# Layer 0 of a two-layer image kernel: real transposes, sums of squares on ScalarE, and another order of the stages in a slot

## The chip, the cores and the metric

The kernel runs on one core of a Trainium2 chip. A core has five engines that run their own instruction streams in order and wait for each other through semaphores: TensorE (PE: matmuls; PEld is its weight load), VectorE (DVE), ScalarE (ACT), GpSimd (POOL) and SyncE (SP, which here issues most of the DMAs). TensorE writes to PSUM, from where VectorE and ScalarE read; GpSimd works in SBUF. The metric is the device time of one execution in microseconds (us), lower is better.

## The reference, cut to what matters

Eight images of 128 x 128 positions with 128 channels go through two layers. Layer 0 is linear attention with a normalization at its end:

```python
qkv = jnp.einsum('bhwc,cf->bhwf', x, w_qkv)
q, k, v = jnp.split(qkv, 3, axis=-1)          # each (B, 4 heads, 32, N), N = 128*128
q = jax.nn.softmax(q, axis=-2) * inv_scale    # over the 32 of a head
k = jax.nn.softmax(k, axis=-1)                # over all N positions
context = jnp.einsum('bhdn,bhen->bhde', k, v)
attn = jnp.einsum('bhde,bhdn->bhen', context, q)
out = jnp.einsum('bhwf,fc->bhwc', attn, w_out) + b_out
mu = jnp.mean(out, axis=-1, keepdims=True)
var = jnp.mean(jnp.square(out - mu), axis=-1, keepdims=True)
out = (out - mu) * jax.lax.rsqrt(var + LN_EPS) * gamma + beta
return out + x
```

Layer 1 is a convolution followed by four selective scans, a gate, a normalization and a projection. The change doesn't touch it.

## The kernel before, in words

Three stages follow each other: `layer0` (the first 2350 us), `layer1_front` (the convolution) and `layer1_scan`, the longest. `layer0` writes two tensors to memory: its result x1, and zs, the gate of layer 1 (Silu of x times half of layer 1's input weights).

An image of layer 0 is cut into 32 groups of 512 positions (`NG`, four columns of 128). Two things are done to each image: `context(b)`, which makes the 128 x 128 context out of keys and values, and afterwards `attend(b)`, which runs the queries through it. `image(b)` interleaves `attend(b)` with `context(b + 1)`, so that all engines have work of both. Its loop runs over slots t; each slot calls each stage once, for a group that lags by a fixed number: `at(scale, t - 2)`, `at(query, t)` and so on, where a = t - 1 counts the groups of the next image. The loop runs 39 slots. There is an image -1 with a context alone, and image 7 with attention alone, in which the gates of the last two images (`gate_group`) run inside the slots; the other images' gates run as one burst after slot 0.

The order of the calls in a slot is the order of the instructions: `in_order` chains all instructions of an engine as they were written. So a stage that is called earlier stands earlier in the queue of every engine it uses, and an instruction that waits holds back all that is behind it on its engine.

The stages of a group (lines of the kernel before):

- query (L266 to L272): TensorE pq = wq * x; VectorE takes the maximum of each head (qm) and subtracts it (q).
- exponent (L275): ScalarE, exp of q in place. normalize (L280 to L282): VectorE sums and inverts (qs), GpSimd multiplies.
- through_wo (L288, L290): four pairs of matmuls that multiply q by Wo, position by position, which also turns positions onto the partitions' side; ScalarE copies pg to gt.
- through_context (L294 to L298): TensorE po = context * gt; VectorE adds the bias (o); ScalarE squares o (sq).
- variance (L302): VectorE sums the squares over the 128 channels, four sums a partition.
- scale (L308 to L313): GpSimd makes rstd out of the four sums, by a power of -0.5 (L310), and d, four diagonal matrices: the identity times rstd.
- turn (L321): TensorE multiplies o by d, four 128 x 128 blocks, which turns o and scales it at once. A matmul in fp32 is two instructions in the profile.
- finish (L325 to L330): ScalarE applies gamma and beta (x1t), GpSimd adds x in place, and every second group a DMA stores two groups.

And of the next image: key (L180, copied by ScalarE to k, L182), larger (L190 to L197: running maximum over four groups on VectorE), fold (every fourth group; L206: a transposition by TensorE, then on VectorE the maximum m, the correction a and the diagonal dg, L208 to L214), spread (L219: a matmul spreads the maximum over the partitions, pmx; L221: ScalarE's exp of a), value (L225, L226), subtract (L231, VectorE), raise_to (L234, ScalarE's exp), add (L240: four pairs of matmuls sum k times v in pc; every fourth group VectorE folds pc into total, L247).

PSUM tiles with the tag "ps" share six buffers in turn, seven tiles a slot in every fourth slot and six otherwise.

The order of a slot before:

```python
            at(scale, t - 2)
            at(finish, t - 3)
            at(query, t)
            at(through_wo, t - 1)
            at(exponent, t)
            ...
            at(turn, t - 2)
            at(spread, a - 1)
            at(variance, t - 1)
```

Of the kernel before, what the change touches and what calls it, by code (L numbers as in the profile page):

```python
# [16 lines left out]
P = 128  # L17
# [7 lines left out]
GW = 4  # L25
GN = GW * H
NG = W // GW
BK = 4
# [49 lines left out]
def layer0(ctx: ExitStack, tc, xT, w_qkv, w_out, b_out, gamma, beta, win, x1, zs):  # L78
# [19 lines left out]
    ident = const.tile([P, P], F32, name="ident")  # L98
# [40 lines left out]
    def group(b, g):  # L139
        return xs[b % 2][:, g * GW : (g + 1) * GW, :]  # L140
# [6 lines left out]
    def gate_group(b, g):  # L147

        v = group(b, g)
        if ORDER[b] % K >= 2:  # L150
            v = wp.tile([P, GW, P], F32, name="v", tag="o", bufs=3)
            nc.vector.tensor_copy(
                v, xs[b % 2].rearrange("p w h -> p h w")[:, g * GW : (g + 1) * GW, :]
            )
        for c in range(NC2):
            pz = ps.tile([P, GW, P], F32, name="pz", tag="ps")
            nc.tensor.matmul(pz, wz[:, c * P : c * P + P], v, start=True, stop=True)
            z = wp.tile([P, GW, P], F32, name="z", tag="k", bufs=7)
            nc.scalar.activation(z, pz, AF.Silu)
            dst = zs[ORDER[b], c][:, g * GN : g * GN + GN]  # L160
            nc.sync.dma_start(dst, z.rearrange("p w h -> p (w h)"))

    def gate(b):

        turned = ORDER[b] % K >= 2
        more = b + 2 < B
        for g in range(NG):
            gate_group(b, g)
            if more and not turned and g % 4 == 3:
                load(b + 2, [g // 4])  # L170
        if more and turned:
            load(b + 2)
# [88 lines left out]
    def attend(b):  # L261

        cn = ctxs[b % 2]
        qs, gs, os, vs, ys = {}, {}, {}, {}, {}

        def query(g):  # L266
            pq = ps.tile([P, GW * NH, HD], F32, name="pq", tag="ps")
            nc.tensor.matmul(pq, wq[:, 0:P], group(b, g), start=True, stop=True)
            qm = sm.tile([P, GW * NH, 1], F32, name="qm")
            nc.vector.tensor_reduce(qm, pq, AX.X, ALU.max)  # L270
            qs[g] = q = wp.tile([P, GW * NH, HD], F32, name="q", bufs=3)
            nc.vector.tensor_tensor(q, pq, qm.to_broadcast([P, GW * NH, HD]), ALU.subtract)  # L272

        def exponent(g):
            nc.scalar.activation(qs[g], qs[g], AF.Exp)  # L275

        def normalize(g):
            q = qs[g]
            t = sm.tile([P, GW * NH, 1], F32, name="qs")
            nc.vector.tensor_reduce(t, q, AX.X, ALU.add)  # L280
            nc.vector.reciprocal(t, t)  # L281
            nc.gpsimd.tensor_tensor(q, q, t.to_broadcast([P, GW * NH, HD]), ALU.mult)  # L282

        def through_wo(g):
            q = qs.pop(g).rearrange("p (w n) d -> p w (n d)", w=GW)
            pg = ps.tile([P, GW, P], F32, name="pg", tag="ps")
            for i in range(GW):
                nc.tensor.matmul(pg[:, i, :], q[:, i, :], wo, start=True, stop=True)  # L288
            gs[g] = gt = wp.tile([P, GW, P], F32, name="gt")
            nc.scalar.copy(gt, pg)  # L290

        def through_context(g):
            po = ps.tile([P, GW, P], F32, name="po", tag="ps")
            nc.tensor.matmul(po, cn, gs.pop(g), start=True, stop=True)  # L294
            os[g] = o = wp.tile([P, GW, P], F32, name="o", bufs=3)
            nc.vector.tensor_tensor(o, po, bb, ALU.add)  # L296
            vs[g] = sq = wp.tile([P, GW, P], F32, name="sq")
            nc.scalar.activation(sq, o, AF.Square)  # L298

        def variance(g):  # L300
            var = sm.tile([P, GW], F32, name="var")
            nc.vector.tensor_reduce(var, vs[g], AX.X, ALU.add)  # L302
            vs[g] = var

        def scale(g):

            var = vs[g]
            nc.gpsimd.tensor_scalar(var, var, 1.0 / P, EPS0, ALU.mult, ALU.add)  # L308
            rstd = sm.tile([P, GW, 1], F32, name="rstd")
            nc.gpsimd.tensor_tensor(rstd[:, :, 0], var, half, ALU.pow)  # L310
            vs[g] = d = wp.tile([P, GW, P], F32, name="d")
            i3 = ident.rearrange("p (o c) -> p o c", o=1)
            nc.gpsimd.tensor_tensor(  # L313
                d, i3.to_broadcast([P, GW, P]), rstd.to_broadcast([P, GW, P]), ALU.mult
            )

        def turn(g):
            o, d = os.pop(g), vs.pop(g)
            ys[g] = pt = ps.tile([P, GW, P], F32, name="pt", tag="ps")
            for i in range(GW):  # L320
                nc.tensor.matmul(pt[:, i, :], o[:, i, :], d[:, i, :], start=True, stop=True)  # L321

        def finish(g):
            y = wp.tile([P, GW, P], F32, name="x1t")
            nc.scalar.activation(y, ys.pop(g), AF.Identity, bias=gb[:, 1:2], scale=gb[:, 0:1])  # L325
# [6 lines left out]
        return query, exponent, normalize, through_wo, through_context, variance, scale, turn, finish  # L332

    def image(b):

        key = larger = fold = spread = value = subtract = raise_to = add = None
        query = exponent = normalize = through_wo = through_context = None
        variance = scale = turn = finish = None
        later = LATER if b >= 0 else 0
        if b + 1 < B:  # L340
            key, larger, fold, spread, value, subtract, raise_to, add = context(b + 1)
        if b >= 0:
            (query, exponent, normalize, through_wo, through_context, variance, scale, turn,
             finish) = attend(b)

        def at(stage, g):
            if stage is not None and 0 <= g < NG:
                stage(g)

        for t in range(later + NG + BK + 2):  # L350
            a = t - later
            at(scale, t - 2)
            at(finish, t - 3)
            at(query, t)
            if b == B - 1 and t < NG:
                gate_group(b - 1, t)
            at(through_wo, t - 1)
            if b == B - 1 and 4 <= t < NG + 4:
                gate_group(b, t - 4)
            at(exponent, t)  # L360
            at(subtract, a - BK - 1)
            at(raise_to, a - BK - 1)
            at(key, a)
            at(normalize, t)
            at(fold, a - 1)
            at(value, a - BK - 1)
            at(larger, a)
            at(through_context, t - 1)
# [841 lines left out]
```

## Time and profile before

| | |
|---|---|
| median of 3 runs | 9565.71 us (9555.7 to 9566.26) |
| profiled execution, span | 9556.3 us |
| layer 0 | about the first 2350 us |
| PE busy, whole span | 6281.6 us, 66% |
| DVE busy, whole span | 8129.7 us, 85% |
| ACT busy, whole span | 7202.0 us, 75% |
| POOL busy, whole span | 7192.2 us, 75% |

The profiled execution is told by its span, from its first instruction to its last. The span lies 9.4 us under the median of the runs, within 1 us of the fastest run. Shares over the whole span mix the three stages: in the scans VectorE and GpSimd are nearly always busy, in layer 0 TensorE is. What the change is worth is to be read from layer 0 alone.

In the profile, L321 is line 321 of the kernel; "pt<-d,o" is a tile written out of the tiles d and o; "128x512" is partitions by elements; "[1.29 <-DVE dg L214]" is idle time before an instruction and the one whose end released it. Matmuls are pipelined, so the step from start to start says more than the length of one.

### The profile page before, as it was taken

What the parts mean: (1) busy time and instruction counts of PE and PEld (TensorE: products, weight loads), DVE (VectorE), ACT (ScalarE), POOL (GpSimd) and SP (SyncE); (2) the same over time, 40 slices, a digit from 0 to 9 for tenths busy, and PEclk for the clock granted to TensorE, in tenths of its full rate; (3) what the DMA queues carried; (4) which work ended last, traced back from release to release, by engine and by line L of the source; (5) the groups of instructions that cost most, each with busy time, mean ns of one, the idle gap of its engine ahead of it and who ended that gap; (6) DMA issues with size and microseconds to landing.
All of it is one profiled execution on the core that took longest, in us unless ns stands there. A gap on an engine that the chain in (4) does not pass through costs nothing. (4 is left out here: it accounts for less than half of the span.)

```text
span 9556.3 us, 89734 instructions
## 1 busy us (share of the span) xinstructions
PE 6281.6 (66%) x24190; PEld 3101.4 (32%) x24352; DVE 8129.7 (85%) x8188; ACT 7202.0 (75%) x8288; POOL 7192.2 (75%) x4361
## 2 busy tenths in 40 slices
PE   8999999898977788777823544636345363543636
PEld 5556655554322233222300311404123040220403
DVE  6667765564988889888979999999999999999996
ACT  5556555567877788777878788888888888888884
POOL 3445544455665578776859999999999999999997
PEclk9999999999988899888955665757557585665857
DMA  2332233313476678987765957759487685867858
GB/s 91 135 133 81 95 133 132 133 71 140 172 266 232 229 262 247 266 263 269 243 204 165 257 174 207 240 174 269 154 228 219 186 260 165 244 190 198 245 165 212
DMA packets 1034807, 1851.21 MB, mean 194 GB/s; under 512 B 274852, under 2 KB 500772, under 8 KB 1026112
## 3 DMA queue, kind: packets, MB, share of 16 engines
q1 hardware_dynamic: 999488, 1711.23, 54.2%
q0 software_dynamic: 34816, 134.23, 7.3%
q8 instruction: 199, 3.26, 0.1%
q14 instruction: 304, 2.49, 0.1%
HBM read 1153.03 MB, written 692.12 MB: 193 GB/s over the span
## 5 line engine op out<-in xcount | busy, mean ns | idle before, releaser
L893 POOL TENSOR_TENSOR ubt<-ubt,sp 128x1024 f32<-128x1024 f32 x1024 | 2457.9, 2458 | 161.0 <-ACT sp L886 74.3
L882 PE MATMUL px<-rows,dtw 128*128 128x512 bf16 x1893 | 909.5, 573 | 2271.7 <-DVE y L943 1063.5
L515 POOL TENSOR_TENSOR tap<-tap 128x1024 f32<-128x1024 f32 x512 | 1206.1, 2367 | 640.1 <-ACT tap L513 517.9
L523 DVE SCALAR_TENSOR_TENSOR acc<-xb,cw,acc 128x1024 f32<-128x1024 f32 x1024 | 1320.6, 1290 | 52.7 <-ACT tap L513 0.9
L886 ACT ACTIVATE sp<-px 128x1024 f32<-128x1024 f32 x1024 | 1046.0, 1024 | 420.7 <-PE px L882 265.6
L951 POOL TENSOR_TENSOR y<-y,ubt 128x512 f32<-128x512 f32 x768 | 1160.0, 1557 | 142.9 <-DVE ubt L924 141.9
L505 PE MATMUL acc<-xi,wt 128*128 128x512 f32 x2048 | 952.2, 608 | 383.9 <-ACT ures L530 383.6
L903 DVE TENSOR_TENSOR_SCAN ubt<-px,ubt 128x1024 f32<-128x1024 f32 x512 | 1177.0, 2332 | 25.9 <-POOL ubt L893 19.2
L901 DVE TENSOR_TENSOR_SCAN ubt<-px,ubt 128x1024 f32<-128x1024 f32 x512 | 1178.3, 2332 | 14.1 <-POOL ubt L893 6.3
L882 PEld LDWEIGHTS <-dtw 128*128 128x128 bf16 x2048 | 163.9, 109 | 3066.2 <-issue 865.9
L890 ACT ACTIVATE px<-sp,sa 128x1024 f32<-128x1024 f32 x1024 | 1110.2, 1109 | 6.1
L513 ACT ACTIVATE tap<-xb,cw 128x1024 f32<-128x1024 f32 x768 | 834.0, 1139 | 68.1 <-POOL tap L515 67.8
L282 POOL TENSOR_TENSOR q<-q,qs 128x512 f32<-128x512 f32 x256 | 271.2, 1060 | 691.5 <-DVE qs L281 691.5
L886 ACT ACT_TABLE_LOAD x512 | 656.9, 1283 | 164.5 <-PE px L882 129.2
L505 PEld LDWEIGHTS acc<-xi,wt 128*128 128x128 f32 x2048 | 383.6, 192 | 928.3 <-ACT ures L530 486.1
L890 ACT ACT_TABLE_LOAD x512 | 656.9, 1283 | 9.2
L1016 PEld LDWEIGHTS px<-wg,z 128*128 128x128 f32 x4096 | 553.8, 218 | 118.6 <-issue 113.5
L909 PE MATMUL pc<-rows,csel 128*128 128x512 bf16 x1017 | 512.7, 585 | 88.9 <-DVE rstd L1004 79.9
L1016 PE MATMUL px<-wg,z 128*128 128x128 f32 x4096 | 554.1, 301 | 0.0
L478 PE MATMUL pxb<-xi,wi 128*128 128x512 f32 x1024 | 495.9, 606 | 4.3 <-ACT xb L487 4.3
L943 DVE TENSOR_TENSOR y<-y,px 128x1024 f32<-128x1024 f32 x384 | 468.7, 1221 | 14.7 <-DVE px L931 0.5
L298 ACT ACTIVATE sq<-o 128x512 f32<-128x512 f32 x256 | 161.2, 630 | 418.2 <-DVE o L296 416.9
(155 smaller groups left out, 15187.7 us busy)
## 6 DMA issues: line engine op xcount, KB each, us to landing
ubt<-ubs SPq DMA_DIRECT2D x512, 1024.0 KB
zs<-z SPq DMA_DIRECT2D x512, 256.0 KB
ubs<-ures SPq DMA_DIRECT2D x256, 512.0 KB
ubs<-turned SPq DMA_DIRECT2D x256, 512.0 KB
z<-zs SPq DMA_DIRECT2D x256, 512.0 KB
y<-gs POOLq DMA_DIRECT2D x128, 1024.0 KB, 10.5
rows<-xps SPq DMA_DIRECT2D x1536, 60.0 KB
xi<-x SPq DMA_DIRECT2D x120, 576.0 KB
```

Of the source, the lines that this page charges most:

```text
L505: nc.tensor.matmul(acc[:, s, :], wt[:, j, c, :], x, start=(j == 0), stop=(j == len(ON_PE) - 1))
L513: nc.scalar.activation(t, at(n, c, *d), AF.Copy, scale=cw[:, c, tap(*d) : tap(*d) + 1])
L515: nc.gpsimd.tensor_tensor(sums[n, c], sums[n, c], t, ALU.add)
L523: nc.vector.scalar_tensor_tensor(acc, at(n, c, *d), cw[:, c, tap(*d) : tap(*d) + 1], acc, ALU.mult, ALU.add)
L882: nc.tensor.matmul(p[:, hf * 512 : hf * 512 + 512], sl.dw[:, c * P : c * P + P], src, start=True, stop=True)
L886: nc.scalar.activation(t, da[n, c], AF.Softplus)
L890: nc.scalar.activation(da[n, c], sp[n, c], AF.Exp, scale=sa[:, sl.s, c : c + 1])
L893: nc.gpsimd.tensor_tensor(ubt[n][:, c, :], ubt[n][:, c, :], sp.pop((n, c)), ALU.mult)
L901: nc.vector.tensor_tensor_scan(e[:, ::-1], x[:, ::-1], e[:, ::-1], start, ALU.mult, ALU.add)
L903: nc.vector.tensor_tensor_scan(e, x, e, start, ALU.mult, ALU.add)
L951: nc.gpsimd.tensor_tensor(v[:, c], v[:, c], h[:, c], ALU.add)
L1016: nc.tensor.matmul(po[:, w, :], z[:, c, w * H : w * H + H], wg[:, c, :], start=(c == 0), stop=(c == NC2 - 1))
```

## The change

Four things in layer 0:

1. The squares: in place of one ScalarE instruction over 128 x 512 and a sum by VectorE (stage variance, which goes), four ScalarE instructions over 128 x 128, each of which also writes the sum of its squares to one column of var (accum_out). The squares themselves are written to a tile of one buffer that nobody reads.
2. The scaling: GpSimd multiplies o itself by rstd, in place, and makes no diagonal matrix.
3. The turn: TensorE transposes the four blocks of o (`nc.tensor.transpose`, a matmul in transpose mode against the identity) in place of multiplying them by d.
4. The order of the calls in a slot. TensorE's is now query, (spread), key, value, Wo, (fold), adding, context, turn. spread is called one slot later than before, right behind query. raise_to comes behind key and value, and through_wo behind all of these; add comes ahead of through_context.

ScalarE's queue in a slot was x1t, gt, exponent of q, exponent of k, copy of k, copy of v, square; it becomes x1t, exponent of q, copy of k, copy of v, exponent of k, gt, four squares. In image 7 it was x1t, two z, gt, two z, exponent, square; it becomes x1t, two z, exponent, gt, two z, four squares. GpSimd's queue and that of the DMAs keep their order.

```diff
-            vs[g] = sq = wp.tile([P, GW, P], F32, name="sq")
-            nc.scalar.activation(sq, o, AF.Square)
-
-        def variance(g):
-            var = sm.tile([P, GW], F32, name="var")
-            nc.vector.tensor_reduce(var, vs[g], AX.X, ALU.add)
-            vs[g] = var
+            sq = wp.tile([P, GW, P], F32, name="sq", bufs=1)
+            vs[g] = var = sm.tile([P, GW], F32, name="var")
+            for i in range(GW):
+                nc.scalar.activation(sq[:, i, :], o[:, i, :], AF.Square, accum_out=var[:, i : i + 1])
 
         def scale(g):
 
-            var = vs[g]
+            var = vs.pop(g)
             nc.gpsimd.tensor_scalar(var, var, 1.0 / P, EPS0, ALU.mult, ALU.add)
             rstd = sm.tile([P, GW, 1], F32, name="rstd")
             nc.gpsimd.tensor_tensor(rstd[:, :, 0], var, half, ALU.pow)
-            vs[g] = d = wp.tile([P, GW, P], F32, name="d")
-            i3 = ident.rearrange("p (o c) -> p o c", o=1)
-            nc.gpsimd.tensor_tensor(
-                d, i3.to_broadcast([P, GW, P]), rstd.to_broadcast([P, GW, P]), ALU.mult
-            )
+            o = os[g]
+            nc.gpsimd.tensor_tensor(o, o, rstd.to_broadcast([P, GW, P]), ALU.mult)
 
         def turn(g):
-            o, d = os.pop(g), vs.pop(g)
+            o = os.pop(g)
             ys[g] = pt = ps.tile([P, GW, P], F32, name="pt", tag="ps")
             for i in range(GW):
-                nc.tensor.matmul(pt[:, i, :], o[:, i, :], d[:, i, :], start=True, stop=True)
+                nc.tensor.transpose(pt[:, i, :], o[:, i, :], ident)
...
             at(query, t)
+            at(spread, a - 2)
             if b == B - 1 and t < NG:
                 gate_group(b - 1, t)
+            at(exponent, t)
+            at(subtract, a - BK - 1)
+            at(key, a)
+            at(value, a - BK - 1)
+            at(raise_to, a - BK - 1)
+            at(normalize, t)
+            at(larger, a)
             at(through_wo, t - 1)
             if b == B - 1 and 4 <= t < NG + 4:
                 gate_group(b, t - 4)
-            at(exponent, t)
-            at(subtract, a - BK - 1)
-            at(raise_to, a - BK - 1)
-            at(key, a)
-            at(normalize, t)
             at(fold, a - 1)
-            at(value, a - BK - 1)
-            at(larger, a)
+            at(add, a - BK - 2)
             at(through_context, t - 1)
-            at(add, a - BK - 2)
             at(turn, t - 2)
-            at(spread, a - 1)
-            at(variance, t - 1)
```

More of the change, by code (lines that the diff above doesn't have):

```diff
@@ L330, in finish @@
                 nc.sync.dma_start(x1[ORDER[b]][:, (g - 1) * GN : (g + 1) * GN], t)
-        return query, exponent, normalize, through_wo, through_context, variance, scale, turn, finish
+        return query, exponent, normalize, through_wo, through_context, scale, turn, finish
     def image(b):
@@ L337, in image @@
         query = exponent = normalize = through_wo = through_context = None
-        variance = scale = turn = finish = None
+        scale = turn = finish = None
         later = LATER if b >= 0 else 0
@@ L342, in image @@
         if b >= 0:
-            (query, exponent, normalize, through_wo, through_context, variance, scale, turn,
+            (query, exponent, normalize, through_wo, through_context, scale, turn,
              finish) = attend(b)
```

## The prediction

> **What bounds the kernel now.** I read the windows view by stage, then TensorE's timeline, then ScalarE's groups and timeline, then both engines in image 7. The change touches layer 0 alone, about the first 2350 of 9556 us.
>
> ```profile
> 2050.00:2355.00 305.00, 253.58 (x963) 136.34 (x961) 118.61 (x213) 235.11 (x335) 152.15 (x169) 0.98 0.37 140
> 300.00:600.00 300.00, 276.58 (x1240) 171.47 (x1240) 211.51 (x361) 180.00 (x314) 154.06 (x172) 0.98 0.30 114
> ```
>
> Columns: window, length, then busy time of matmuls, weight loads, VectorE, ScalarE, GpSimd, and the granted clock. In an ordinary image TensorE is 92% busy at clock 0.98, ScalarE 60%. In image 7, which runs the gate in its slots, no engine is full.
>
> ```profile
> 452.89 0.27 PE L206 MATMUL pmt<-ident,run 128*128 128x128 f32 x1
> 453.00 1.02 PE L225 MATMUL pv<-x,wq 128*128 128x512 f32 x2
> ...
> 458.19 0.49 PE L219 MATMUL pmx<-dg,ones 128*128 128x128 f32 x2 [1.29 <-DVE dg L214]
> 458.51 1.02 PE L268 MATMUL pq<-x,wq 128*128 128x512 f32 x2
> ...
> 484.96 1.02 PE L268 MATMUL pq<-x,wq 128*128 128x512 f32 x2
> ```
>
> TensorE's timeline: start, length, operation. Four slots take 484.96 - 458.51 = 26.45 us. In the same view three of the four take 6.11 each and TensorE never waits in them: the starts step by 0.86 (each projection), 0.89 (each of Wo, adding, turn). The fourth takes 7.8 to 8.2, with the 1.29 wait on dg shown. Over the slots in which all stages run (query 6 to query 31, 25 slots), an image takes 163.3 us, 6.53 a slot. One transposition (pmt) gives the array to the next matmul after 0.11.
>
> ```profile
> 500.42 0.63 ACT L234 ACTIVATE k<-k 128x512 f32<-128x512 f32 x1
> 500.95 0.57 ACT L182 COPY k<-pk 128x512 f32<-128x512 f32 x1
> 501.42 0.59 ACT L226 COPY vt<-pv 128x512 f32<-128x512 f32 x1
> 504.44 0.63 ACT L298 ACTIVATE sq<-o 128x512 f32<-128x512 f32 x1 [2.42 <-DVE o L296]
> 504.97 0.76 ACT L325 ACTIVATE x1t<-pt,gb 128x512 f32<-128x512 f32 x1
> 505.63 0.57 ACT L290 COPY gt<-pg 128x512 f32<-128x512 f32 x1
> ```
>
> ScalarE overlaps neighbours by about 0.1: from start to start an exponent or square is 0.53, a copy 0.47, x1t 0.66. Today gt comes right after x1t, so Wo's result is copied long before "context" needs it.
>
> ```profile
> L221 ACT ACTIVATE a<-a 128x1 f32<-128x1 f32 x56 | 10.8, 192 | 0.0
> L491 ACT COPY xb<-xb 128x128 f32<-128x128 f32 x4 | 1.2, 298 | 0.1
> ```
>
> These are the nearest rows to a square over 128 elements and to the reading of one sum per partition (third number from the end: mean ns of one). In the timeline such a copy is followed 0.20 later, such a one-element activation 0.09 later.
>
> ```profile
> 2191.65 1.28 ACT L275 ACT_TABLE_LOAD   x1
> 2192.94 0.63 ACT L275 ACTIVATE q<-q 128x512 f32<-128x512 f32 x1
> 2195.16 0.63 ACT L298 ACTIVATE sq<-o 128x512 f32<-128x512 f32 x1 [1.59 <-DVE o L296]
> ```
>
> Image 7 on ScalarE: a table load, which works on the engine's own state, overlaps with nothing (1.29 to the exponent after it). From exponent to exponent its slots take 8.69.
>
> **The change, part by part.** All sums are made against the profiled span, 9556.3; the median run, 9565.7, lies 9.4 above it, and I add that at the end. What can be told from no change is about 0.2%, 19 us.
>
> *Turn.* Eight matmuls (0.89) become four transpositions: 4 x 0.11 = 0.44. That takes 0.45 a group off TensorE, 115 us over 256 groups if TensorE stayed the bound. Upper bound: the transpositions at the old 0.89, that is, no gain.
>
> *Spread a slot later, behind query.* dg then has a whole slot; the 1.29 wait goes. TensorE's own work falls to query, key, value, context 4 x 0.86, Wo and adding 2 x 0.89, turn 0.44: 5.66 a slot, 5.75 with a quarter of pmt (0.11) and pmx (0.22). The exponent of a (0.09) moves along.
>
> *Variance's reduction leaves VectorE* (0.69 a slot). VectorE is not the bound here; GpSimd's product o*rstd has the shape of ident*rstd (1.04). Both at nothing: GpSimd's 4.6 a slot sit under 6.5. The DMAs keep their number and order on SP's queue.
>
> *Squares.* One activation (0.53) becomes four over 128 elements with an accumulator; no run shows an accumulator's price. Call the four S. Low end: 4 x 0.20 = 0.82, the sum for nothing. With a sum that is read by an instruction like the 128x1 row and overlaps fully: 4 x 0.29 = 1.18. Without overlap: 4 x (0.298 + 0.192) = 1.96. High end, a read as dear as the whole copy: 4 x 0.596 = 2.38. I take 1.96: the accumulator is state of the engine, like the table, and the trace's instruction on such state overlaps with nothing.
>
> The Trainium skill, "ScalarE: Activation LUTs", section "What ACT_TABLE_LOAD costs", has 186 ns + 0.833 ns per element and an overlap of 93 ns; for 128 elements that is an estimated 0.20 from start to start, as in the trace. It prices no accumulator; by it alone S would be 0.80 and the forecast the first rival's.
>
> *The new order.* ScalarE's queue is now x1t, exponent of q, copy k, copy v, exponent of k, gt, squares. "Context" (po) waits for gt; behind po on TensorE stand turn and the next query. Two loops result.
>
> Loop A, through query: pq to its end 1.02, max 0.68, subtraction 0.69, three handoffs of 0.03 to 0.04: the exponent starts 2.50 after pq. Then 0.53 + 0.47 + 0.47 + 0.53 to gt, gt 0.585: 5.09. Handoff 0.05: po starts at 5.14, though TensorE would be free at 4.36 (0.86 x 3 + 0.89 x 2). po to turn 0.96 (as after a waited-for po in image 7), turn 0.44: 6.54 from query to query. Today's mean is 6.53: what turn and dg give, gt takes back.
>
> Loop B, through the squares: exponent start to po start 2.00 + 0.585 + 0.05 = 2.64; po to its end 1.13 (it waited), handoff 0.04, o 0.67, handoff 0.03: squares start at 4.51. Then S, then x1t 0.66, then the next exponent: 5.17 + S. With S = 1.96: 7.13. It binds from S = 1.37.
>
> So for 7 images x 25 slots: (7.13 - 6.53) x 175 = +105. Slots 2 to 5 without value and adding: about 25.3 for 24.8, +3. The end of an image: slot 31 is a full one (+0.9), and the last turn, which already waits 2.50 for GpSimd, gets its sums S after o instead of 0.63 + 0.03 + 0.69 = 1.35 after it (+0.6): 1.5 x 7 = +11. Image -1, eight waits of 0.3 on dg gone: -2.
>
> Image 7: the loads stay two a slot. Today's 8.69 is a loop through ScalarE, in which it idles 1.59 before the square. In the new order it need not: x1t 0.66, z 0.48, z 0.63, load 1.29, exponent 0.53, gt 0.60, load 1.29, z 0.48, z 0.48: 6.44 + S = 8.40. Times 28 slots: -8.
>
> Sum: 105 + 3 + 11 - 2 - 8 = +109. 9565.7 + 109 = 9675, slower by 1.1%.
>
> A rule that speaks against the transposition itself: the Trainium skill, "TensorE: Matmul & The Clock Gate", section "Part 4: PE-mode transpose", gives about 275 ns for one in a kernel and says that it doesn't count as work for the clock gate. The trace has 0.27 as pmt's length, but 0.11 to its follower, at clock 0.98. Were the 275 the step, turn would take 1.10, and an estimate of loop A 7.20.
>
> **The rivals.**
>
> *The sums are cheap* (the other side). S of 0.82 to 1.18. Mechanism: ScalarE's accumulator costs its instruction little. Loop A binds, 6.54: nothing in images 0 to 6; image 7 at 7.62 (S = 1.18): -30; image -1: -2; together about -30, 9536. At S = 0.82 another loop of image 7 (exponent to gt to po to squares) holds it at 7.30: -41, 9525. For it: neighbouring 128x128 copies do overlap. Against it: the read needs its own activation's sum. It decides below S = 1.48, where 175 x (S - 1.36) + 28 x (S - 2.25) is zero.
>
> *Half overlap*: the read waits for its square, but the next square overlaps: 4 x 0.395 = 1.58. Loop B 6.75: 39 + 3 - 2 - 19 = +21, 9587.
>
> *Dear sums*: S = 2.38, loop B 7.55: 179 + 10 + 17 + 4 - 2 = +208, 9774.
>
> *Gt is not late*, and the change does on TensorE what its parts say: 5.75 a slot, (5.75 - 6.53) x 175 = -137; with image 7 at S = 1.18 (-30) 9399. Against it: the exponent of q can't start before 2.50, and four instructions stand between it and gt's end.
>
> **How the numbers follow.** S near 1.96 0.48, dear 0.14, half overlap 0.14, cheap 0.22, gt not late 0.02. The likeliest alone: S from 1.8 to 2.15, 9645 to 9710. The range of 8 in 10 takes in half overlap and the cheap case down to S about 1.0, and half the way to the dear one: 9530 to 9745. Faster 0.25 (cheap, gt not late, the low edge of half overlap); same 0.06; slower 0.69.
>
> **What would show it.** Right: query starts 7.1 apart in the middle of images 0 to 6 and 8.4 in image 7; pmx without a wait on dg; TensorE waiting for gt before po about 1.4 in each slot; ScalarE without a gap from the squares over x1t to the exponent; squares 0.49 apart. Turn: four transpositions 0.11 apart. The forecast is wrong if the squares stand 0.3 apart or closer (then 6.54 a slot and a gap before the exponent), or 0.6 (then 7.5); if the granted clock falls below 0.98; or if po starts without waiting.

## The result and the profile after

The changed kernel takes 9589.87 us (median of six runs, 9585.03 to 9595.75); the kernel before takes 9560.14 on the same chip (six runs, 9546.26 to 9566.26). The ratio is 1.0035, with a 95% interval of 1.0023 to 1.0046: slower by 0.35%, about 30 us. The forecast was 9675, slower by 109 us. The direction came true and the time lies in the range, but the size is off by a factor of more than three, and the reason that the forecast gave for it is not the one that holds.

The profiled execution after has a span of 9593.9 us, before 9556.3: 37.6 more. I cut layer 0 of both traces at the starts of the query (pq), which each image has 32 of. Times in us, each image's stretch rounded to 0.1 and then summed over the images, so that a sum can be 0.2 off:

| stretch | before | after | difference | forecast |
|---|---|---|---|---|
| image -1, up to the first query | 110.4 | 110.3 | -0.1 | -2 |
| query 0 to 1 (with the burst of gates) | 387.8 | 390.0 | +2.2 | 0 |
| query 1 to 2 | 62.4 | 83.1 | +20.7 | 0 |
| query 2 to 6 | 178.6 | 178.0 | -0.6 | +3 |
| query 6 to 31 (25 full slots) | 1142.6 | 1186.2 | +43.6 | +105 |
| query 31 to the next image's query 0 | 180.6 | 186.4 | +5.8 | +11 |
| image 7 | 286.6 | 257.4 | -29.2 | -8 |
| everything behind layer 0 | 7207.1 | 7202.4 | -4.7 | 0 |

The windows view by stage (window, length, then busy time of matmuls, weight loads, VectorE, ScalarE, GpSimd, the granted clock, the DMAs' share and GB/s), after:

```profile
300.00:600.00 300.00, 257.83 (x1057) 152.25 (x1057) 191.33 (x311) 186.63 (x523) 147.97 (x162) 0.97 0.30 114
2100.00:2390.00 290.00, 248.07 (x916) 132.27 (x915) 116.14 (x198) 263.38 (x604) 161.72 (x179) 0.98 0.38 145
```

In an ordinary image TensorE falls from 92% busy to 86% (257.83 of 300): it has less work in each slot and waits more. In image 7 ScalarE rises from 77% (235.11 of 305) to 91% (263.38 of 290). ScalarE's groups of layer 0 (busy time, mean ns of one, then idle time ahead of it) show what a sum costs:

```profile
L300 ACT ACTIVATE sq<-o 128x128 f32<-128x128 f32 x1024 | 303.3, 298 | 520.5 <-DVE o L296 520.5
L300 ACT ACTIVATION_READ_ACCUMULATOR sq<-o 128x1 f32 x1024 | 192.3, 188 | 0.0
```

Each square with a sum is two instructions: the square itself (298 ns) and a read of the accumulator (188 ns). These are the two durations that the forecast took. It added them up. The timeline of a slot, the same place as the one shown of before (start, length, operation), shows that they don't add up:

```profile
505.15 1.02 PE L268 MATMUL pq<-x,wq 128*128 128x512 f32 x2
505.77 0.31 ACT L300 ACTIVATE sq<-o 128x128 f32<-128x128 f32 x1 [2.07 <-DVE o L296]
505.99 0.19 ACT L300 ACTIVATION_READ_ACCUMULATOR sq<-o 128x1 f32 x1
506.08 0.29 ACT L300 ACTIVATE sq<-o 128x128 f32<-128x128 f32 x1
506.21 0.69 DVE L270 TENSOR_REDUCE qm<-pq 128x16 f32<-128x512 f32 x1 [0.54 <-PE pq L268]
...
506.96 0.76 ACT L319 ACTIVATE x1t<-pt,gb 128x512 f32<-128x512 f32 x1
507.01 0.69 DVE L272 TENSOR_TENSOR q<-pq,qm 128x512 f32<-128x512 f32 x1
507.73 0.63 ACT L275 ACTIVATE q<-q 128x512 f32<-128x512 f32 x1
...
509.74 0.58 ACT L290 COPY gt<-pg 128x512 f32<-128x512 f32 x1
510.38 1.12 PE L294 MATMUL po<-gt,ctxn 128*128 128x512 f32 x2 [0.70 <-ACT gt L290]
511.34 0.60 PE L315 MATMUL pt<-ident,o 128*128 128x128 f32 x4
511.78 1.02 PE L268 MATMUL pq<-x,wq 128*128 128x512 f32 x2
```

The read starts 0.22 after its square, the next square 0.09 after the read, and x1t comes 1.19 after the first square: S is about 1.18 (4 x 0.295). There is a gap of 0.11 between x1t's step (0.66) and the exponent, so the squares don't hold the exponent up in this slot. The slot takes 511.78 - 505.15 = 6.63, and TensorE waits in it, 0.70 on gt, which is what the new order was expected to do. In TensorE's waits from 300 to 2060 us (total, times, longest) this is the largest:

```profile
PE po L294 <- ACT gt L290: 162.0, 182, 7.2
PE pk L180 <- DMA x<-in_x: 21.7, 4, 5.6
```

So the slot is loop A of the forecast, at 6.63 where 6.54 was worked out. In steady state the four slots take 6.63, 6.63, 6.89 and 6.87; before, they took 6.11 three times and about 7.8.

Two more readings. The first is a slot in which VectorE folds the running maximum (after, timeline):

```profile
489.45 1.10 DVE L196 TENSOR_TENSOR run<-run 128x256 f32<-128x256 f32 x1
490.23 1.23 POOL L282 TENSOR_TENSOR q<-q,qs 128x512 f32<-128x512 f32 x1
490.59 1.02 DVE L197 TENSOR_TENSOR run<-run 128x128 f32<-128x128 f32 x1
491.53 0.68 DVE L296 TENSOR_TENSOR o<-po,bb 128x512 f32<-128x512 f32 x1
492.30 0.31 ACT L300 ACTIVATE sq<-o 128x128 f32<-128x128 f32 x1 [2.47 <-DVE o L296]
...
494.25 0.62 ACT L275 ACTIVATE q<-q 128x512 f32<-128x512 f32 x1
```

The fold takes 2.1 on VectorE ahead of the addition o; ScalarE idles 2.47 for it, so the squares, x1t and the exponent come late. This exponent starts 7.02 after the one before it. In the kernel before, the same two instructions took 1.13 and 0.29 at this place (502.28 and 503.45). What differs for the second is GpSimd: here its product q (490.23 to 491.46) is under way when the maximum starts. In the twelve kernels that have this maximum over 128 x 128 (the two here and ten of the experiments below) it took 0.29 in all 346 cases in which no GpSimd instruction ran beside it. It took 1.01 to 1.25 in the other 422, and in each of those a GpSimd product or addition over 128 x 512 was under way at its start. No run moved GpSimd's work alone.

The second is the start of an image, slot 1. First the kernel before, then after:

```profile
398.76 1.05 PE L288 MATMUL pg<-wo,q 128*128 128x128 f32 x8
...
403.97 2.05 PE L180 MATMUL pk<-x,wq 128*128 128x512 f32 x2 [4.16 <-DMA x<-in_x]
405.81 1.91 PE L294 MATMUL po<-gt,ctxn 128*128 128x512 f32 x2
```

```profile
411.92 2.04 PE L180 MATMUL pk<-x,wq 128*128 128x512 f32 x2 [5.53 <-DMA x<-in_x]
413.75 1.91 PE L288 MATMUL pg<-wo,q 128*128 128x128 f32 x8
416.34 2.08 PE L294 MATMUL po<-gt,ctxn 128*128 128x512 f32 x2 [0.68 <-ACT gt L290]
```

The first key of the next image waits for the load of x in both. Before, Wo had already run when this wait began, and context could follow at once. After, Wo stands behind the wait, so Wo, its copy gt and context all come after it. Matmuls right after the wait have twice their usual length (Wo 1.91 for 1.05). This makes query 1 to 2 in images 0 to 6 20.7 us longer in all, and no term of the forecast had it.

### The profile page after: what moved, and what is told of

It is laid out like the page before. It is cut to its first block, busy times and chain, and to the rows that moved or that the text cites. A ratio compares the mean times of both kernels' runs of the same rounds, so it can differ in the third digit from the quotient of the medians.

```text
span 9593.9 us, 89267 instructions
## 1 busy us (share of the span) xinstructions
PE 6208.7 (65%) x23166; PEld 3007.2 (31%) x23328; DVE 8033.6 (84%) x7932; ACT 7322.1 (76%) x10080; POOL 7201.9 (75%) x4361
## 5 line engine op out<-in xcount | busy, mean ns | idle before, releaser
L300 ACT ACTIVATE sq<-o 128x128 f32<-128x128 f32 x1024 | 303.3, 298 | 520.5 <-DVE o L296 520.5
## 6 DMA issues: line engine op xcount, KB each, us to landing
y<-gs POOLq DMA_DIRECT2D x128, 1024.0 KB, 10.4
```

## The experiments

My theory after the result: S is 1.18, so the squares' loop doesn't bind. What makes the kernel slower is the place of through_wo, which puts gt at the end of ScalarE's queue (loop A) and Wo behind the load at an image's start. The gains of the other parts are real but smaller than that. The rivals are written with each expectation. Slot times below are starts from query to query in the middle of image 2, unless said otherwise; "25 slots" is query 6 to 31, the mean of images 0 to 6. Each ratio is against the kernel before on the same chip as the run, where its median was 9553.7, 9558.4 or 9559.0 (9560.1 above); so medians of different experiments compare to within some 6 us.

### Wo back behind the query

```diff
             if b == B - 1 and t < NG:
                 gate_group(b - 1, t)
+            at(through_wo, t - 1)
+            if b == B - 1 and 4 <= t < NG + 4:
+                gate_group(b, t - 4)
             at(exponent, t)
...
             at(larger, a)
-            at(through_wo, t - 1)
-            if b == B - 1 and 4 <= t < NG + 4:
-                gate_group(b, t - 4)
             at(fold, a - 1)
```

> The changed kernel with one call moved: through_wo goes back to its old place behind query. Theory (the place of gt on ScalarE is the price): po no longer waits for the exponent of q, the loop of 6.63 from query to query is cut, TensorE runs slots of 5.7 to 6.6, held only where VectorE folds the maximum; about 6.25 on average, (6.25 - 6.77) x 175 = -90 against the changed kernel, and another -20 since the first pk of an image no longer stands ahead of Wo: about 9480. Image 7 stays near 7.6 a slot. Rival 1 (the sums on ScalarE or the transpositions are the price): no change, 9590.

Measured: 9541.62, ratio 0.9986 (0.9976 to 0.9996). The 25 slots take 159.3 against 169.4 after: this one stage's place costs 10.1 an image, 71 us over seven. Query 1 to 2 falls from 83.1 to 71.2 in all. That carries the theory. Most of the miss (9480 had been expected) is image 7, which takes 305.8 in place of 257.4: ScalarE's slot there went up to 9.40, where 7.6 had been expected. The rest is mainly the slots, 6.37 on average where 6.25 had been expected. ScalarE's timeline in image 7:

```profile
2156.68 0.63 ACT L275 ACTIVATE q<-q 128x512 f32<-128x512 f32 x1
...
2158.96 0.31 ACT L300 ACTIVATE sq<-o 128x128 f32<-128x128 f32 x1 [1.65 <-DVE o L296]
```

With the exponent at the end of the queue again, ScalarE idles 1.65 ahead of the squares, as it did before the change (1.59), and the four sums come on top: 8.69 + (1.18 - 0.53) = 9.34. So in image 7 the new place of Wo is a gain of about 1.8 a slot, while in images 0 to 6 it is a loss.

### The old squares in the changed kernel

One square over 128 x 512 and VectorE's reduction (stage variance, at the slot's end) come back; the new order, turn and spread stay.

```diff
-            sq = wp.tile([P, GW, P], F32, name="sq", bufs=1)
-            vs[g] = var = sm.tile([P, GW], F32, name="var")
-            for i in range(GW):
-                nc.scalar.activation(sq[:, i, :], o[:, i, :], AF.Square, accum_out=var[:, i : i + 1])
+            vs[g] = sq = wp.tile([P, GW, P], F32, name="sq")
+            nc.scalar.activation(sq, o, AF.Square)
```

> The changed kernel with the old single square (128x512) and VectorE's sum at the end of the slot. Rival 1 (ScalarE is burdened by the sums: 495 us of squares and reads for 161 before): ScalarE gets 0.65 a slot back, so up to -110, about 9480. Theory: ScalarE has room, and VectorE's sum comes back into a loop: exponent to po 2.64, po 1.13, o 0.71, square 0.66, sum 0.72, qm 0.78, q 0.72: 7.3 a slot, (7.3 - 6.77) x 175 = +93, with image 7 some 10 to 20 shorter: about 9665.

Measured: 9720.61, ratio 1.0171 (1.0156 to 1.0186); slots of 7.44. A change that takes ScalarE's instructions from four pairs to one makes the kernel 131 us slower than after. The timeline shows why:

```profile
502.59 1.02 PE L268 MATMUL pq<-x,wq 128*128 128x512 f32 x2
503.49 0.63 ACT L298 ACTIVATE sq<-o 128x512 f32<-128x512 f32 x1 [2.35 <-DVE o L296]
504.15 0.69 DVE L302 TENSOR_REDUCE var<-sq 128x4 f32<-128x512 f32 x1 [1.03 <-ACT sq L298]
504.75 0.68 DVE L270 TENSOR_REDUCE qm<-pq 128x16 f32<-128x512 f32 x1
...
508.91 1.12 PE L294 MATMUL po<-gt,ctxn 128*128 128x512 f32 x2 [1.79 <-ACT gt L290]
```

The reduction waits for the square, and the maximum of the query (qm) waits behind it on VectorE: qm starts 2.16 after the query, against 1.06 in the changed kernel. Through the exponent and gt this lands in po, which waits 1.79. So in the new order the sums by ScalarE are a gain of about 0.7 a slot. The forecast had costed the reduction's leaving "at nothing", because VectorE isn't the bound. That reason was wrong: in the new order the reduction would stand ahead of the query's maximum, on the chain that the order lengthens. The forecast time doesn't suffer by it, since loops A and B were added up without the reduction.

### The new order alone

Kernel before with the new order of the calls (variance last in the slot), the old squares and the old turn.

```diff
             at(query, t)
+            at(spread, a - 2)
...
-            at(through_wo, t - 1)
...
             at(key, a)
...
+            at(raise_to, a - BK - 1)
+            at(normalize, t)
             at(larger, a)
-            at(through_context, t - 1)
+            at(through_wo, t - 1)
...
+            at(fold, a - 1)
             at(add, a - BK - 2)
+            at(through_context, t - 1)
             at(turn, t - 2)
-            at(spread, a - 1)
             at(variance, t - 1)
```

> The kernel before in the new order as the only change; old turn, old squares, VectorE's sum at the end of the slot. Theory: both loops bind, through gt with a turn of 0.89 at 7.1, through VectorE's sum at 7.3: (7.3 - 6.53) x 175 = +135, the starts of the images +20, image 7 down from 8.69 to 7.0 to 7.3 (-40 to -45): about +110, 9670. Rival 1 (the order is harmless, the sums are the price): 9560 or less.

Measured: 9722.37, ratio 1.0174 (1.0159 to 1.0189); slots of 7.37. The order alone is a loss of 1.7%, about 50 more than expected: image 7 takes 7.74 a slot where 7.0 to 7.3 had been expected, and the 25 slots take 184.7 (7.39 on average for 7.3). With the old squares, the new turn makes no difference to the total (9720.61 with, 9722.37 without), but only because two parts cancel: with it image 7 is shorter (248.4 for 262.1) and the 25 slots are longer (186.3 for 184.7).

### The old turn in the changed kernel

GpSimd makes d again, and TensorE multiplies by it.

```diff
-            nc.gpsimd.tensor_tensor(o, o, rstd.to_broadcast([P, GW, P]), ALU.mult)
+            vs[g] = d = wp.tile([P, GW, P], F32, name="d")
...
-                nc.tensor.transpose(pt[:, i, :], o[:, i, :], ident)
+                nc.tensor.matmul(pt[:, i, :], o[:, i, :], d[:, i, :], start=True, stop=True)
```

> The changed kernel with the old turn (matmuls by a diagonal d). Theory: turn stands in the loop query, exponent, gt, po, turn, query, so its 0.45 comes on top of 6.63: 7.08 a slot; (7.08 - 6.77) x 175 = +54, image 7 (held by ScalarE) unchanged: about 9645. Rival 3 (transpositions are no gain here, or TensorE's work is not on the path): 9590 or less.

Measured: 9657.32, ratio 1.0107 (1.0092 to 1.0122); slots of 7.09. TensorE's timeline, one slot's ends:

```profile
503.20 1.02 PE L268 MATMUL pq<-x,wq 128*128 128x512 f32 x2
...
509.39 1.05 PE L318 MATMUL pt<-d,o 128*128 128x128 f32 x8
510.28 1.02 PE L268 MATMUL pq<-x,wq 128*128 128x512 f32 x2
```

Turn takes 0.89 again and a plain slot is longer by 0.46: in the new order turn lies wholly on loop A, so its step is paid in full. This agrees with the 0.44 that the four transpositions take in the timeline. All four slots take 7.09, so the two late ones grow by 0.2 only, and the 25 slots go from 169.4 to 177.2.

### The turn alone

Kernel before with o scaled by GpSimd and the transpositions; old order, old squares.

```diff
-            vs[g] = d = wp.tile([P, GW, P], F32, name="d")
...
+            o = os[g]
+            nc.gpsimd.tensor_tensor(o, o, rstd.to_broadcast([P, GW, P]), ALU.mult)
...
-                nc.tensor.matmul(pt[:, i, :], o[:, i, :], d[:, i, :], start=True, stop=True)
+                nc.tensor.transpose(pt[:, i, :], o[:, i, :], ident)
```

> The kernel before with the turn as transpositions (and o scaled in place) as the only change; old squares, old order. TensorE's work falls by 0.45 a slot. Theory: three slots of four fall from 6.11 to 5.66, but the fourth, which waits for dg on VectorE, grows by most of it, to 8.8; image 7 is held by ScalarE and stays at 8.69: about -20, 9540. Rival 2 (TensorE's work is what counts): -0.45 x 256 = -115, 9445. Rival 3 (transpositions are slow or cost clock): slower than before, over 9580, and a granted clock under 0.98 in layer 0.

Measured: 9578.34, ratio 1.0026 (1.0017 to 1.0035): slower, where faster had been expected. Three plain slots take 5.66 as they should, 0.45 less than before. But one slot in four grew to 8.4 to 9.0, and often the plain slot behind it to 7.3; the 25 slots take 165.9 for 163.3. TensorE's timeline:

```profile
487.19 0.66 PE L318 MATMUL pt<-ident,o 128*128 128x128 f32 x4
489.63 0.49 PE L219 MATMUL pmx<-dg,ones 128*128 128x128 f32 x2 [1.79 <-DVE dg L214]
489.95 1.80 PE L268 MATMUL pq<-x,wq 128*128 128x512 f32 x2
491.55 1.92 PE L288 MATMUL pg<-wo,q 128*128 128x128 f32 x8
493.26 1.13 PE L180 MATMUL pk<-x,wq 128*128 128x512 f32 x2
```

TensorE comes to pmx 0.45 earlier and waits that much longer for dg (1.79). Then query and Wo run at half rate: 3.31 for the two (489.95 to 493.26) instead of 1.75. By the records of the granted clock, layer 0 has 42 stretches at half clock, 180 us in all, against 17 and 89 us in the kernel before. Of the 42, 22 begin within 1 us of the end of such a wait for dg (1.78 to 1.80), each 3.4 long. In the kernel before, none of the 42 waits for dg in layer 0 of 1.0 to 1.3 was followed by one.

### The turn alone, with spread a slot later

Two causes could lower the clock: the transpositions themselves, or the long wait right behind them. The same kernel as the one above, with only this moved:

```diff
             at(query, t)
+            at(spread, a - 2)
...
             at(turn, t - 2)
-            at(spread, a - 1)
             at(variance, t - 1)
```

> The kernel before with the turn as transpositions and spread a slot later, behind query; old squares, rest of the order old. Theory: half clock came from the wait for dg right behind the transpositions; without that wait no step of a query is over 1.0 in the middle of an image, the clock between 420 and 600 us is 0.99 to 1.00 again, 25 slots in 160 to 163 for 166 with the turn alone: 9535 to 9555. Rival (the transpositions themselves take the clock down wherever they stand): 0.97 again, and no faster than 9578.

Measured: 9554.55, ratio 0.9998 (0.9989 to 1.0008). The windows view from 420 to 600 us, first the turn alone, then with spread moved:

```profile
420.00:600.00 180.00, 162.76 (x745) 100.60 (x744) 147.49 (x254) 106.81 (x191) 122.34 (x137) 0.97 0.13 52
```

```profile
420.00:600.00 180.00, 164.80 (x763) 98.51 (x762) 149.45 (x259) 108.87 (x195) 124.06 (x140) 1.00 0.12 46
```

The same transpositions run with the granted clock at 1.00. So the transpositions alone don't lower it; the loss came with the long wait behind them (pmx still waits for dg here, 0.9 at most and behind the query). Moving spread recovers 24 us of the turn's loss. The 0.45 that turn saves still doesn't come through: the slots take 5.89, 6.64, 7.07 and 6.56 (163.0 for 25). TensorE's largest wait from 300 to 2060 us is now Wo's for the normalized query, 49.0 us in 77 waits.

### The sums alone

Kernel before with the four accumulating squares only.

```diff
-            vs[g] = sq = wp.tile([P, GW, P], F32, name="sq")
-            nc.scalar.activation(sq, o, AF.Square)
...
+            vs[g] = var = sm.tile([P, GW], F32, name="var")
+            for i in range(GW):
+                nc.scalar.activation(sq[:, i, :], o[:, i, :], AF.Square, accum_out=var[:, i : i + 1])
...
-            at(variance, t - 1)
```

> The kernel before with the sums on ScalarE as the only change; old turn, old order. Theory: TensorE's 6.11 a slot stays, VectorE loses 0.69 ahead of dg, so the wait for dg in the fourth slot falls by about 0.5: 25 slots in 159 to 160 for 163.3, -25; image 7 is a loop through ScalarE and gets the sums' extra 0.65 to 0.7 in each of its slots, 9.4 for 8.69, +20: together -10 to 0, 9550. Rival 1 (the sums are the price of the change): +0.65 in each slot, over 9650.

Measured: 9552.66, ratio 0.9991 (0.9982 to 1.0000), too near to no change to be told from it. Its parts are larger than the total. The 25 slots fall from 163.3 to 159.9 (three of 6.11 and one of 7.39), since VectorE, without the reduction, gets to dg earlier: pmx's wait on dg falls from 43.2 us in all to 23.9. Image 7 gives most of it back, at 9.40 a slot for 8.69.

### Sums and turn in the old order

The changed kernel with the calls in the order of before:

```diff
             at(query, t)
-            at(spread, a - 2)
...
+            at(through_wo, t - 1)
...
             at(exponent, t)
             at(subtract, a - BK - 1)
-            at(key, a)
-            at(value, a - BK - 1)
             at(raise_to, a - BK - 1)
+            at(key, a)
             at(normalize, t)
-            at(larger, a)
-            at(through_wo, t - 1)
...
             at(fold, a - 1)
-            at(add, a - BK - 2)
+            at(value, a - BK - 1)
+            at(larger, a)
             at(through_context, t - 1)
+            at(add, a - BK - 2)
             at(turn, t - 2)
+            at(spread, a - 1)
```

> The changed kernel in the old order (spread again at the end of its slot): turn and sums without the order. Theory: three slots of 5.66 and one that waits for dg, 7.7: 6.2 on average, (6.2 - 6.53) x 175 = -58; image 7 at 9.4, +20; if the clock falls behind the wait for dg as in the kernel with the turn alone, another 1.0 to 1.5 in each fourth slot, +45 to +65: 9520 to 9585, less than the changed kernel. Rival 1 (sums or turn are the price): 9590 or more.

Measured: 9523.79, ratio 0.9964 (0.9951 to 0.9976), faster by 0.36%. The slots are three of 5.66 and one of 8.3 (157.1 for 25). Here too the transpositions stand right ahead of the wait on dg, but the clock stays at 0.99 from 420 to 600 us. TensorE's waits on dg in four kernels (total, times, longest): before, the turn alone, the sums alone, and sums and turn:

```profile
PE pmx L219 <- DVE dg L214: 43.2, 42, 1.3
```

```profile
PE pmx L219 <- DVE dg L214: 70.1, 43, 1.8
```

```profile
PE pmx L219 <- DVE dg L214: 23.9, 39, 0.8
```

```profile
PE pmx L219 <- DVE dg L214: 52.7, 42, 1.4
```

Sums and turn help each other: the sums free VectorE, so dg comes earlier and the wait behind the transpositions stays at 1.4 at most. From here to the changed kernel only the order differs, and that step costs 66 us (9589.87 - 9523.79), though it removes the wait on dg (one of 0.8 is left).

### Wo ahead of the first key

For the start of an image: Wo ahead of the key in that one slot.

```diff
+            if a == 0:
+                at(through_wo, t - 1)
             at(key, a)
...
-            at(through_wo, t - 1)
+            if a != 0:
+                at(through_wo, t - 1)
```

> The changed kernel, but in the first slot of an image's keys (a = 0) through_wo is called ahead of key. Theory: Wo and context of group 0 no longer stand behind a pk that waits for the load of x; the step from query 1 to query 2 falls from 12.6 to 12.9 back to 9.6 to 10.1 in images 1 to 4, some 15 to 20 in all over the images, and nothing else moves. Rival (the longer step comes from the sums or from gt's place): still above 12.

Measured in one run: 9571.08, span 9569.3. Query 1 to 2 falls to 10.0 to 10.1 in images 1 to 4, from 83.1 to 72.4 in all, so half of the 20.7 is won back; images 5 and 6 (12.1 and 10.4, for 6.1 and 7.5 before the change) do less well, and why stays open. The 25 slots stay at 169 to 170. One run can't tell the kernel's time to 10 us, and the reading rests on the stretch.

### Without the fold of the maximum

This leaves out two instructions and with them a part of the computation (the running maximum over the four columns of a block is not folded into one).

```diff
-            if i == BK - 1:
-                run = runs[j]
-                nc.vector.tensor_tensor(run[:, 0:2], run[:, 0:2], run[:, 2:4], ALU.max)
-                nc.vector.tensor_tensor(run[:, 0], run[:, 0], run[:, 1], ALU.max)
```

> The changed kernel without the two steps that fold the running maximum over its four columns; this leaves three of four columns out of the maximum that the keys' exponent is shifted by. Theory: the slots of 6.9 to 7.0 are those in which VectorE's other work delays the addition o and, through the squares and x1t, the next exponent; one of the two long steps in four goes back to 6.63, the other one (dg) stays at 6.9: about 6.69 on average. Rival (pmt and pmx on TensorE make the long slots): both stay.

Measured in one run: 9563.92, span 9562.1. Slots of 6.63, 6.63, 6.63 and 6.87: one of the two late slots is gone, and the 25 slots fall by 15.6 us over seven images (1186.2 to 1170.6). The other late slot stays, and in it VectorE makes m, a and dg ahead of the addition o.

### Two orders

The runs point to a kernel with the new order in image 7 only. In the others, key, Wo and value are spread so that gt comes third in ScalarE's queue.

```diff
+            if b < B - 1:
+                at(scale, t - 2)
+                at(spread, a - 2)
+                at(subtract, a - BK - 1)
+                at(finish, t - 3)
+                at(query, t)
+                at(fold, a - 1)
+                at(key, a)
+                at(through_wo, t - 1)
+                at(exponent, t)
+                at(value, a - BK - 1)
+                at(larger, a)
+                at(normalize, t)
+                at(add, a - BK - 2)
+                at(raise_to, a - BK - 1)
+                at(through_context, t - 1)
+                at(turn, t - 2)
+            else:
...
```

> The three new parts with two orders: image 7 in the changed kernel's order, the others in the order scale, spread, subtract, finish, query, fold, key, through_wo, exponent, value, larger, normalize, add, raise_to, context, turn. Theory: with gt ahead of the exponent and VectorE's folding spread over the slot no loop is longer than TensorE's own 5.75; 5.8 to 6.1 a slot for 6.53, -75 to -130, image 7 at 7.6 for 8.69, -25: 9405 to 9460. Rival: VectorE's chain from o to the next exponent holds it at the 6.37 that was measured with Wo behind query: 9490 to 9500.

Measured: 9431.64, ratio 0.9868 (0.9852 to 0.9885), faster than both kernels by 1.3% and 1.7%. TensorE's timeline:

```profile
502.02 1.02 PE L268 MATMUL pq<-x,wq 128*128 128x512 f32 x2
502.88 1.02 PE L180 MATMUL pk<-x,wq 128*128 128x512 f32 x2
503.74 1.05 PE L288 MATMUL pg<-wo,q 128*128 128x128 f32 x8
504.63 1.02 PE L225 MATMUL pv<-x,wq 128*128 128x512 f32 x2
505.49 1.06 PE L240 MATMUL pc<-vt,k 128*128 128x129 f32 x8
506.38 1.02 PE L294 MATMUL po<-gt,ctxn 128*128 128x512 f32 x2
507.24 0.60 PE L315 MATMUL pt<-ident,o 128*128 128x128 f32 x4
507.68 1.02 PE L268 MATMUL pq<-x,wq 128*128 128x512 f32 x2
...
510.13 1.16 PE L288 MATMUL pg<-wo,q 128*128 128x128 f32 x8 [0.46 <-POOL q L282]
```

A plain slot is 5.66, TensorE's own work to the hundredth: no step waits. The fourth slot is 6.72: it holds pmt and pmx besides, and Wo waits 0.46 in it for the q that GpSimd normalizes (last line). The 25 slots take 147.3 (5.89 a slot), and image 7 stays at 7.61 a slot. The same three changes of operations are worth 1.3% in this order and cost 0.35% in the one that was made. Wo ahead of the first key was not tried in it; query 1 to 2 still takes 12.7 to 13.3 in most images there.

## Why the prediction was right or wrong

**The step that failed is S = 1.96**, the four squares "without overlap: 4 x (0.298 + 0.192)". The durations were right (298 and 188 ns). The reason for adding them, that "the accumulator is state of the engine, like the table", was an analogy with the table load, and it doesn't hold: a read overlaps with its square and with the next square as other neighbours do, and S is 1.18. That was the value named there for full overlap, and with it the premise of the first rival. Loop B is then 5.17 + 1.18 = 6.35, below loop A. By the starts in the slot shown after the change it comes to 6.52 (the exponent starts 0.11 after x1t's step ends), still below. So the path was wrong as well: the forecast had loop B hold every slot at 7.13, and the plain slot is loop A, through gt. The forecast named this as a sign of being wrong: squares 0.3 apart or closer, and a gap before the exponent. It named a clock below 0.98 as another; from 300 to 600 us that is 0.97 after, but 0.99 from 420 to 600, inside one image.

The Trainium skill, "ScalarE: Activation LUTs", section "What ACT_TABLE_LOAD costs", by whose instruction price S would have been 0.80, comes nearer than my analogy: a square to the instruction behind it takes 0.20 to 0.22 here. The rest of S is the second instruction that a sum brings, 0.09 more each.

**S alone doesn't explain the size.** With 1.18 the first rival's sum was -30, 9536, and the measured +30 lies 60 on the other side. Three things were missing, the first two of them in the 25 slots:

- Loop A is 6.63, not 6.54. Nearly all of the difference is one handoff: from the maximum to the subtraction on VectorE it is 0.80 from start to start (506.21 to 507.01) for an instruction of 0.69, where I took length and a handoff of 0.03 to 0.04. The row was in the trace of before (505.70 to 506.49). 0.09 x 175 slots is 16 us.
- Two slots of four are late, at 6.87 to 6.89, because VectorE does the work that comes once in four groups ahead of o, and squares, x1t and exponent then run late behind it. The mean of the four is 0.13 above 6.63, 175 times: 22 us. Taking out the fold showed 15.6 of this and of the remainder below (the one late slot by itself makes 0.26 x 175 / 4 = 11). That the other late slot comes from m, a and dg was read in the timeline and not tried by itself.
- Query 1 to 2: +20.7, Wo and context behind the wait for the load of x. The forecast moved Wo past the first key without asking what that key waits for. Putting Wo ahead of it won half back, in images 1 to 4 nearly all.

16 + 22 and the 2 that loop A at 6.54 already had over 6.53 make 40 of the 43.6 in the full slots. The remaining 4 and the few us at the gates are not assigned; the rest of the program varied between 7195 and 7213 us over the kernels, though nothing in it was changed.

**Image 7** was forecast from the right chain (6.44 + S). With S = 1.18 that is 7.62, and it measured 7.61, so its 28 steps fall from 241.5 to 216.5.

**What held.** The turn is 4 x 0.11 = 0.44. The Trainium skill, "TensorE: Matmul & The Clock Gate", section "Part 4: PE-mode transpose", gives about 275 ns for one; that is its length here (0.27 for pmt) and not its step. The wait on dg is gone, but for one of 0.8. Po waits for gt in nearly every slot (182 waits from 300 to 2060 us), 0.70 in a plain one (the 1.4 that was forecast belonged to loop B). "What turn and dg give, gt takes back" is what the runs show: sums and turn in the old order are 0.36% faster than before, and the new order turns that into 0.35% slower. The rival that gt is not late falls for this order, and its slot of 5.75 is nearly reached (5.89) in the order in which gt is copied third.

**What was costed at nothing and wasn't**: the reduction's leaving VectorE. In the new order it is worth 0.7 a slot, since the query's maximum would stand behind it. The sum of the forecast was right without the term, as its loops had no reduction in them.

**What was right by accident**: the sign. The forecast put it on dear sums. It lies in the order, and by the forecast's own break-even (S of 1.48) a correct S would have made it say faster.

**Open:** why the clock falls to half behind a wait of 1.8 after the transpositions, and not in the kernel with sums and turn, where it waits up to 1.4. The traces narrow it. I counted TensorE's waits in layer 0 of all thirteen kernels, leaving out those around which the clock was at half already, and asked how often half clock began within about 1 us of a wait's end:

| behind | length of the wait | waits | followed by half clock |
|---|---|---|---|
| ordinary matmuls | 1.70 to 1.85 | 29 | 0 |
| ordinary matmuls | 2.0 to 2.5 | 121 | 51 |
| the four transpositions | 1.20 to 1.45 | 42 | 0 |
| the four transpositions | 1.78 to 1.80 | 42 | 22 |

So a long wait is enough without transpositions, and behind them a shorter one was. Each row on transpositions comes from one kernel (sums and turn; the turn alone), and no run varied the wait alone.

## What to carry to other kernels

In a slot loop whose engines run in order, work out every loop that comes back to the same instruction, from start-to-start steps in the trace and not from lengths plus a guessed handoff, and put the copy that the next matmul needs early in its engine's queue. Ask of each stage that is moved what it now stands behind, in the first slot of an image as well as in the middle: one wait for a load cost half as much here as all the full slots together. An order that suits one stage of a program (image 7) can be a loss in another, and the same edits were worth -1.3% or +0.35% by the order alone.

## What the runs showed of the hardware

- A sum by ScalarE's accumulator is an instruction of its own, 188 ns long, that starts 0.20 to 0.22 after its square and gives the engine to the next after 0.09. Square over 128 x 128 and sum: 0.295 from start to start.
- Transpositions of 128 x 128 in fp32 follow each other after 0.11 us, about two fifths of what they'd appear to take by length times count (0.44 for 4 x 0.27).
- Behind transpositions and a wait of 1.78 to 1.80 TensorE's granted clock fell to half after 22 of 42 waits, for 3.4 us each time; with spread behind the query the same transpositions ran at 1.00. Behind ordinary matmuls it fell after 51 of 121 waits of 2.0 to 2.5, and after none of 29 of 1.70 to 1.85.
- On VectorE the subtraction of the query's maximum came 0.10 after the end of the maximum that it needs in nearly all groups (0.80 from start to start for 0.69; 243 of 256 before). In the first groups of an image it mostly came 0.03 after, like the reciprocal after the sum that it needs. So needing the result doesn't make the 0.10; what does was not tried.
- A maximum over 128 x 128 on VectorE, in place, took 0.29 us when GpSimd had no instruction under way (346 times in twelve kernels). It took 1.01 to 1.25 when one of GpSimd's products or additions over 128 x 512 was under way at its start (422 times), longer than VectorE's addition over 128 x 512 (0.68).
